# An LSTM step's four gates in one PSUM bank, with one sigmoid and one product for both pairs, in the steps that have FFN work

## The chip, the cores and the metric

The kernel runs on one core of a Trainium2 chip. The metric is the device time of one execution in microseconds. A core has a matrix engine (TensorE, PE in the profile, its weight loads PEld), VectorE (DVE), ScalarE (ACT), GpSimd (POOL) and SyncE (SP), which mostly issues DMAs. Matmul results land in PSUM, in banks of 512 fp32 elements per partition; TensorE writes them, VectorE and ScalarE read them.

## The reference

An LSTM with 256 units runs over 64 steps for 32 sequences, from h0 = `cond_1024`. Its output goes through three dense layers (256 → 1024 → 1024 → 256) whose weights are +1 or −1, and is added to the input `x`:

```python
def step(carry, xw_t):
    prev_h, prev_c = carry
    a = xw_t + prev_h @ Wh
    i = jax.nn.sigmoid(a[:, :Hd])
    f = jax.nn.sigmoid(a[:, Hd:2 * Hd])
    o = jax.nn.sigmoid(a[:, 2 * Hd:3 * Hd])
    g = jnp.tanh(a[:, 3 * Hd:])
    next_c = f * prev_c + i * g
    next_h = o * jnp.tanh(next_c)
    return ((next_h, next_c), next_h)
...
w = jnp.where(kernel_bool, jnp.float32(1.0), jnp.float32(-1.0))
...
x = x + ffn(lstm(x, cond_1024, Wx, Wh, b), k0, k1, k2, s0, s1, s2)
```

The first layer sees h and −h side by side, and the first two layers are followed by relu(.) * 2. All values are fp32.

## The kernel before

**Layout of a step.** The 256 units are cut into four quarters of 64. A tile of a step has 128 partitions, quarter by sequence (4 × 32), and 64 elements. The gates stand in the order candidate, input, forget, output (`GATES`, slots 0 to 3).

**Two stages.** The loop over `t` at the end of the function runs through the 64 steps. In each it issues the gate products (`gates_from_h`, L308), then the cell (`cell_step`, L325 to L342), and then a share of other TensorE work, written out by hand, that fills the time until the next h is there. Before step `X_STEPS` = 21 this is the input product x @ Wx for later steps (`x_products`, L249; results leave PSUM with the bias through L265 into `xg`). From step 21 on it is the FFN over blocks of 16 steps (`ffn`; matmuls at L425, L679, L666 and, for the last two blocks, L452), with 10 or 11 matmuls of 512 elements a step, set by `total_ffn` over the steps left. After step 63 the rest of the FFN runs without a recurrence beside it.

**A step's gates.** `gates_from_h` adds h @ Wh into two PSUM banks: the first three slots into one, 192 wide, the output gate into the other, 64 wide. In each bank there are 2 halves of the contraction by 4 quarters, each a matmul with 32 columns, fp32, which the trace shows as two passes. What is added to lies there already: `gates_from_x` has ScalarE copy the next step's input product into both banks (L319, L320), after the tanh of this step in ScalarE's order.

**A step's cell.** ScalarE: sigmoid of input and forget gate (L325), tanh of the candidate (L326), sigmoid of the output gate from the other bank (L327). VectorE: kept = forget × c (L329), new = input × candidate (L331), c = kept + new (L333). ScalarE: th = tanh(c) (L335). VectorE: h = output × th (L337), then the turn of h by 32 × 32 blocks into `hist` (L342), which the next step's gate products take as weights.

**What else the engines do.** Each engine executes in the order of the program. In FFN steps, behind the cell, ScalarE evicts FFN banks (L368 relu, L436, L437, L514 copy) and rounds h (L361), and VectorE forms the remainders that make the FFN's operands exact (L369, L438, L362), turns outputs (L392) and adds up weight blocks (L418). `load` keeps a count of a step's larger VectorE pieces. GpSimd and the DMAs have little to do after the first 20 us.

Of the kernel before, what the change touches and what calls it, by code (L numbers as in the profile page):

```python
# [34 lines left out]
F32 = mybir.dt.float32  # L35
F32R = mybir.dt.float32r
U8 = mybir.dt.uint8
AF = mybir.ActivationFunctionType
# [5 lines left out]
def lstm_ffn(ctx: ExitStack, tc: tile.TileContext, x, cond, wx_d, wh_d, b_d, k0_d, k1_d, k2_d, s0_d, s1_d, s2_d, out):  # L44
    nc = tc.nc
    P = 128
# [4 lines left out]
    HQ = H // NQ  # L51
# [11 lines left out]
    X_STEPS = 21  # L63
# [13 lines left out]
    cell = ctx.enter_context(tc.tile_pool(name="cell", bufs=2))  # L77
# [6 lines left out]
    def act(shape, dtype, name):  # L84
        return apool.tile(shape, dtype, tag="act", name=name)
# [77 lines left out]
    for i in range(2):  # L163
        t = act([P, 2, F0], U8, f"k0_{i}")
# [102 lines left out]
    def next_x(half):  # L267

        if half < 2 * NB:
            load[0] += 1  # L270
            turn_x(*divmod(half, 2))
            if half + 4 < 2 * NB:
                load_x(*divmod(half + 4, 2), [nc.sync])
# [25 lines left out]
    hist, hparts = {}, {}  # L299

    gate_banks = [ps_g.tile([P, TB], F32, tag=f"gates{n}", name=f"gates{n}") for n in (3, 1)]
    gates = [g[:, : n * HQ].rearrange("p (g j) -> p g j", j=HQ) for g, n in zip(gate_banks, (3, 1))]

    def gates_from_h(t, hT):
        for g, slots in zip(gates, (slice(0, 3), slice(3, 4))):
            for k in range(2):
                for q in range(NQ):
                    nc.tensor.matmul(  # L308
                        g[q * N : (q + 1) * N],
                        hT[:, k, :],  # L310
                        wh_q[:, k, q, slots],
                        start=False,
                        stop=(k == 1),
                        skip_group_check=True,
                    )

    def gates_from_x(t):
        x_t = xg[t // 2 * 2][:, t % 2].rearrange("p (g j) -> p g j", g=4)
        nc.scalar.copy(gates[0], x_t[:, :3])  # L319
        nc.scalar.copy(gates[1], x_t[:, 3:])  # L320

    def cell_step(t, c):
        sig = cell.tile([P, 3, HQ], F32, tag="sig", name=f"sig{t}")
        cand = cell.tile([P, HQ], F32, tag="cand", name=f"cand{t}")
        nc.scalar.activation(sig[:, 0:2, :], gates[0][:, 1:3], AF.Sigmoid)  # L325
        nc.scalar.activation(cand, gates[0][:, 0], AF.Tanh)  # L326
        nc.scalar.activation(sig[:, 2, :], gates[1][:, 0], AF.Sigmoid)  # L327
        kept = cell.tile([P, HQ], F32, tag="kept", name=f"kept{t}")
        nc.vector.tensor_mul(kept, sig[:, 1, :], c)  # L329
        new = cell.tile([P, HQ], F32, tag="new", name=f"new{t}")  # L330
        nc.vector.tensor_mul(new, sig[:, 0, :], cand)  # L331
        c = cell.tile([P, HQ], F32, tag="c", name=f"c{t}")
        nc.vector.tensor_add(c, kept, new)  # L333
        th = cell.tile([P, HQ], F32, tag="th", name=f"th{t}")
        nc.scalar.activation(th, c, AF.Tanh)  # L335
        h = cell.tile([P, HQ], F32, tag="h", name=f"h{t}")
        nc.vector.tensor_mul(h, sig[:, 2, :], th)  # L337
        i, s = divmod(t, SH)
        if s == 0:
            hist[i] = hpool.tile([P, 2, SH * N], F32, tag="hist", name=f"hist{i}")  # L340
        hT = hist[i][:, :, ts(s, N)]
        nc.vector.transpose(hT, h.rearrange("p (j b) -> p b j", b=2))  # L342
        if t + 1 < T:
            gates_from_x(t + 1)
        return c, hT

    def split_h(i):

        b, s = divmod(i, SB // SH)
        if s == 0:  # L350
            hparts[b] = (
                hpool.tile([P, 2, TB], F32R, tag="hhi", name=f"hhi{b}"),
                hpool.tile([P, 2, TB], F32R, tag="hlo", name=f"hlo{b}"),
            )
        hi, lo = (p[:, :, ts(s, SH * N)] for p in hparts[b])
        full = hist.pop(i)
        if b == NB - 1:

            hi, lo = (a.rearrange("p k (n t) -> p k t n", n=N) for a in (hi, lo))
            full = full.rearrange("p k (t n) -> p k t n", n=N)  # L360
        nc.scalar.copy(hi, full)  # L361
        nc.vector.tensor_tensor(lo, full, hi, ALU.subtract)  # L362
# [58 lines left out]
    f, parts = {}, {"b11": {}, "b21": {}}  # L421
# [291 lines left out]
    for half in range(2):  # L713
        load_x(2, half, [nc.sync])
    hT = const.tile([P, 2, N], F32, name="hT_first")
    c = cell.tile([P, HQ], F32, tag="c", name="c_first")
    nc.vector.memset(c, 0.0)  # L717

    def copy_bias():
        p_bias = ps_o.tile([P, 4, HQ], F32, tag="po", name="p_bias")  # L720
# [24 lines left out]
    for _ in x_products(SB // 2, AHEAD):  # L745
        pass
    gates_from_x(0)


    def ffn():  # L750
        for b in range(NB - 2):
            yield from ffn_block(b)
        yield from last_blocks(NB - 2)
# [13 lines left out]
    for t in range(T):  # L767
        load[0] = 0
        gates_from_h(t, hT)
        c, hT = cell_step(t, c)  # L770
        if t % SH == SH - 1:
            splits.append(t // SH)
        if outputs:
            load[0] += 1
            if next(outputs[0], "end") == "end":
                outputs.popleft()
        if t == X_STEPS:
            work, done = ffn(), 0
        goal = (t + 1) * total_x // X_STEPS if t < X_STEPS else (t + 1 - X_STEPS) * total_ffn // (T - X_STEPS)
        while done < goal:  # L780
            left_over[0] = goal - done
            done += next(work)
        if t == X_STEPS - 1:
            next(work, None)

        if turns and load[0] < 2:
            next_x(turns.popleft())
        if splits and (load[0] < 2 or t == T - 1 or t == SH * splits[0] + 2 * SH - 1):
            split_h(splits.popleft())
        else:  # L790
            if t >= FIRST_CHORE and chores:
                part = chores.popleft()()
                if part is not None:
                    w0_parts.append(part)
            elif t >= W2_STEP and chores2:
                chores2.popleft()()
            if w0_parts and (load[0] < 2 or t == X_STEPS - 1):
                w0_parts.popleft()()
            while sum_parts and t >= SUM_STEP and load[0] < 2:
                load[0] += 1  # L800
                sum_parts.popleft()()
# [32 lines left out]
```

## Time and profile before

| | us |
|---|---|
| runs of the kernel | 307.01, 307.42, 308.49 (median 307.42) |
| profiled execution | 307.09 |
| its span | 305.3 |
| PE busy | 299.3 |
| DVE busy | 187.8 |
| ACT busy | 154.9 |
| gate passes of 192 elements, 1008 (steps 1 to 63) | mean 0.330 |
| gate passes of 64 elements, 1008 | mean 0.219 |
| input-product passes of 256 elements, 880 | mean 0.379 |

Duration is from start to modelled end; passes overlap, so durations don't add up to time. A row of the timeline has start, length, engine, line, operation, what it writes and reads, and in brackets how long the engine had been idle before it and what ended that. A row of the chain has start, length and what carried it. The steps begin at 16.5 us (step 0), the FFN steps at 79.9, and the last step's gates at 231.4.

### The profile page before, as it was taken

The page shows a single profiled execution, that of the slowest core. Times are in us where ns is not written, and L with a number is a line of the kernel's source. Part 1 is how long each engine was busy: PE and PEld are TensorE (multiplying, and loading weights), DVE is VectorE, ACT ScalarE, POOL GpSimd, SP SyncE. Part 2 cuts the span into 40 slices and gives each one's busy share as a digit, 9 for nine tenths or more (in the row PEclk, how much of TensorE's full clock was granted, in tenths as well). Part 3 has the DMA queues.
Part 4 walks back from the last instruction along what each step waited for, and adds up shares of the span by engine and source line. Part 5 has one row for each costly group of instructions (what it writes and reads, how often), then busy time and mean ns, then how long its engine had stood idle before and what let it go on. Part 6 is the DMA issues. An engine that isn't in the chain of part 4 may idle for free.

```text
span 305.3 us, 9553 instructions
## 1 busy us (share of the span) xinstructions
PE 299.3 (98%) x4010; PEld 233.8 (77%) x4010; DVE 187.8 (62%) x527; ACT 154.9 (51%) x526; POOL 6.6 (2%) x24
## 2 busy tenths in 40 slices
PE   8999999999999999999999999999999999999993
PEld 4988887787777777777777777777777888888893
DVE  2476767676774565666575746444456689796341
ACT  0224657784565654444453544655676688644100
POOL 5300000000000000000000000000000000000000
PEclk9999999999999999999999999999999999999999
DMA  6865001133000000000001000000001330000012
GB/s 182 210 181 114 20 10 48 32 84 84 4 0 2 2 2 1 2 2 1 2 2 38 19 18 2 0 2 3 3 0 37 91 83 0 0 0 2 0 51 88
DMA packets 27450, 10.87 MB, mean 36 GB/s; under 512 B 23560, under 2 KB 26632, under 8 KB 27408
## 3 DMA queue, kind: packets, MB, share of 16 engines
q1 hardware_dynamic: 24768, 8.66, 11.5%
q10 hardware_dynamic: 2400, 1.57, 1.8%
q8 instruction: 31, 0.51, 0.7%
q0 software_dynamic: 240, 0.04, 0.1%
q14 instruction: 11, 0.09, 0.1%
HBM read 8.16 MB, written 2.10 MB: 34 GB/s over the span
## 4 chain that ended last, share of the span: by engine, by line
PE 98%; DVE 0%; issue 0%
PE p L679 21%; PE gates L308 20%; PE px L249 18%; PE q L452 12%; PE p L425 9%; PE po L666 5%; PE po L629 2%; PE gates L452 2%; PE po L617 2%; PE r L452 2%; PE gates L425 1%; PE p_idle L708 1%; PE gates L706 0%; DVE o L637 0%; PE p_bias L723 0%; DVE idle L113 0%
## 5 line engine op out<-in xcount | busy, mean ns | idle before, releaser
L308 PEld LDWEIGHTS gates<-wh,hist 128*32 128x32 f32 x2016 | 54.6, 109 | 22.3 <-issue 7.8
L308 PE MATMUL gates<-wh,hist 128*32 128x192 f32 x2016 | 68.1, 275 | 0.0
L249 PE MATMUL px<-wx,xT 128*32 128x256 f32 (+1 forms) x1168 | 60.5, 353 | 0.1
L249 PEld LDWEIGHTS px<-wx,xT 128*32 128x32 f32 x1168 | 42.4, 110 | 11.4 <-DVE c_first L717 0.8
L325 ACT ACTIVATE sig<-gates 128x128 f32<-128x128 f32 x64 | 17.7, 277 | 60.7 <-PE gates L308 60.4
L329 DVE TENSOR_TENSOR kept<-sig,c 128x64 f32<-128x64 f32 x63 | 14.2, 225 | 32.4 <-ACT sig L325 32.1
L335 ACT ACTIVATE th<-c 128x64 f32<-128x64 f32 x64 | 16.4, 257 | 32.2 <-DVE c L333 32.2
L337 DVE TENSOR_TENSOR h<-sig,th 128x64 f32<-128x64 f32 x64 | 14.4, 225 | 20.7 <-ACT th L335 20.7
L265 DVE TENSOR_TENSOR xg<-px,bias 128x512 f32<-128x512 f32 x32 | 21.2, 671 | 2.8 <-PE px L249 2.3
L425 PE MATMUL p<-hlo,w 128*128 128x512 f32 x56 | 22.5, 402 | 0.0
L425 PE MATMUL p<-hhi,w 128*128 128x512 f32 x56 | 22.3, 399 | 0.0
L319 ACT COPY gates<-xg 128x192 f32<-128x192 f32 x64 | 20.0, 313 | 0.6 <-DVE xg L265 0.6
L342 DVE STREAM_TRANSPOSE hist<-h 128x64 f32<-128x64 f32 x64 | 15.7, 246 | 2.6
L333 DVE TENSOR_TENSOR c<-kept,new 128x64 f32<-128x64 f32 x64 | 14.4, 225 | 2.2
L327 ACT ACTIVATE sig<-gates 128x64 f32<-128x64 f32 x64 | 14.9, 233 | 0.1
L331 DVE TENSOR_TENSOR new<-sig,cand 128x64 f32<-128x64 f32 x64 | 14.0, 218 | 0.0
L326 ACT ACTIVATE cand<-gates 128x64 f32<-128x64 f32 x64 | 14.0, 218 | 0.0
L320 ACT COPY gates<-xg 128x64 f32<-128x64 f32 x64 | 13.0, 203 | 0.0
L425 PEld LDWEIGHTS p<-hlo,w 128*128 128x128 f32 x56 | 10.5, 188 | 2.5
L425 PEld LDWEIGHTS p<-hhi,w 128*128 128x128 f32 x56 | 10.5, 188 | 2.4
L214 ACT ACTIVATE w<-bits,nsgn,sgn 128x1024 fp32r<-128x1024 uint8 x8 | 9.9, 1241 | 0.0
L362 DVE TENSOR_TENSOR hlo<-hist,hhi 128x256 fp32r<-128x256 f32 x16 | 7.5, 468 | 2.6 <-ACT hhi L361 2.6
(361 smaller groups left out, 573.4 us busy)
## 6 DMA issues: line engine op xcount, KB each, us to landing
x<-in_x_dram SPq DMA_DIRECT2D x52, 64.0 KB, 2.7
out_dram<-o SPq DMA_DIRECT2D x28, 64.0 KB, 1.8
bits<-in_L_ffn_k_dram SPq DMA_DIRECT2D x10, 128.0 KB, 3.4
wx<-in_L_cond_Wx_dram SPq DMA_DIRECT2D x2, 256.0 KB, 4.4
wx<-in_L_cond_Wx_dram ACTq DMA_DIRECT2D x4, 128.0 KB, 5.3
wh<-in_L_cond_Wh_dram ACTq DMA_DIRECT2D x2, 256.0 KB, 6.1
wh<-in_L_cond_Wh_dram SPq DMA_DIRECT2D x2, 256.0 KB, 6.8
k<-in_L_ffn_k_dram SPq DMA_DIRECT2D x2, 256.0 KB, 3.0
```

The costliest lines, as they stand in the source:

```text
L249: nc.tensor.matmul(p[q * N : (q + 1) * N, t % 2, slots], xT[i // 2, i % 2][:, s, k, :], wx_q[:, k, q, slots], start=start, stop=False, ski ...
L265: nc.vector.tensor_tensor(xg[t], p.rearrange("p t g j -> p t (g j)"), b, ALU.add)
L308: nc.tensor.matmul(g[q * N : (q + 1) * N], hT[:, k, :], wh_q[:, k, q, slots], start=False, stop=(k == 1), skip_group_check=True,)
L319: nc.scalar.copy(gates[0], x_t[:, :3])
L325: nc.scalar.activation(sig[:, 0:2, :], gates[0][:, 1:3], AF.Sigmoid)
L327: nc.scalar.activation(sig[:, 2, :], gates[1][:, 0], AF.Sigmoid)
L335: nc.scalar.activation(th, c, AF.Tanh)
L342: nc.vector.transpose(hT, h.rearrange("p (j b) -> p b j", b=2))
L425: nc.tensor.matmul(p, w0[:, k, ts(m, P)], a[:, k, :], start=(n == 0), stop=(n == 3))
L452: nc.tensor.matmul(bank, a(k)[:, ts(i, P)], b[k][n], start=first and k == 0 and n == 0, stop=k == K2 - 1 and n == 1, skip_group_check=True,)
L666: nc.tensor.matmul(po[m], w2[:, m, k], a1[k][n], start=(k == 0 and n == 0), stop=(k == FC1 - 1 and n == 1))
L679: nc.tensor.matmul(p1[m], w1[:, k, ts(m, P)], a0[k][n], start=(k == 0 and n == 0), stop=(k == FC0 - 1 and n == 1),)
```

## The change

It concerns the 43 steps from 21 on. There all four slots lie in the first of the two banks, 256 wide: `gates_from_h` issues 8 matmuls in place of 16, and `gates_from_x` one copy in place of two. The cell takes the tanh of the candidate first and then one sigmoid of input, forget and output gate, 192 wide. The candidate is written beside c, into a tile `pair` that the last step's c is in, so that one multiplication of 128 elements forms input × candidate and forget × c; the sum goes into the next `pair`. In steps 0 to 20 the two banks, three activations and two multiplications stay, with the results in `parts` and `pair`.

```diff
     gate_banks = [ps_g.tile([P, TB], F32, tag=f"gates{n}", name=f"gates{n}") for n in (3, 1)]
-    gates = [g[:, : n * HQ].rearrange("p (g j) -> p g j", j=HQ) for g, n in zip(gate_banks, (3, 1))]
+    rows, last_row = (g.rearrange("p (r j) -> p r j", j=HQ) for g in gate_banks)
+
+    def gate_parts(t):
+
+        if t < X_STEPS:
+            return (rows[:, :3], slice(0, 3)), (last_row[:, :1], slice(3, 4))
+        return ((rows[:, :4], slice(0, 4)),)
 
     def gates_from_h(t, hT):
-        for g, slots in zip(gates, (slice(0, 3), slice(3, 4))):
+        for g, slots in gate_parts(t):
...
-        nc.scalar.copy(gates[0], x_t[:, :3])
-        nc.scalar.copy(gates[1], x_t[:, 3:])
-
-    def cell_step(t, c):
+        for g, slots in gate_parts(t):
+            nc.scalar.copy(g, x_t[:, slots])
+
+    def cell_step(t, pair):
         sig = cell.tile([P, 3, HQ], F32, tag="sig", name=f"sig{t}")
-        cand = cell.tile([P, HQ], F32, tag="cand", name=f"cand{t}")
-        nc.scalar.activation(sig[:, 0:2, :], gates[0][:, 1:3], AF.Sigmoid)
-        nc.scalar.activation(cand, gates[0][:, 0], AF.Tanh)
-        nc.scalar.activation(sig[:, 2, :], gates[1][:, 0], AF.Sigmoid)
-        kept = cell.tile([P, HQ], F32, tag="kept", name=f"kept{t}")
-        nc.vector.tensor_mul(kept, sig[:, 1, :], c)
-        new = cell.tile([P, HQ], F32, tag="new", name=f"new{t}")
-        nc.vector.tensor_mul(new, sig[:, 0, :], cand)
-        c = cell.tile([P, HQ], F32, tag="c", name=f"c{t}")
-        nc.vector.tensor_add(c, kept, new)
+        parts = cell.tile([P, 2, HQ], F32, tag="parts", name=f"parts{t}")
+        cand, c = pair[:, 0], pair[:, 1]
+        if t < X_STEPS:
+            nc.scalar.activation(sig[:, 0:2, :], rows[:, 1:3], AF.Sigmoid)
+            nc.scalar.activation(cand, rows[:, 0], AF.Tanh)
+            nc.scalar.activation(sig[:, 2, :], last_row[:, 0], AF.Sigmoid)
+            nc.vector.tensor_mul(parts[:, 1], sig[:, 1, :], c)
+            nc.vector.tensor_mul(parts[:, 0], sig[:, 0, :], cand)
+        else:
+            nc.scalar.activation(cand, rows[:, 0], AF.Tanh)
+            nc.scalar.activation(sig, rows[:, 1:4], AF.Sigmoid)
+            nc.vector.tensor_mul(parts, sig[:, 0:2], pair)
+        pair = cell.tile([P, 2, HQ], F32, tag="pair", name=f"pair{t}")
+        c = pair[:, 1]
+        nc.vector.tensor_add(c, parts[:, 1], parts[:, 0])
...
-    c = cell.tile([P, HQ], F32, tag="c", name="c_first")
-    nc.vector.memset(c, 0.0)
+    pair = cell.tile([P, 2, HQ], F32, tag="pair", name="pair_first")
+    nc.vector.memset(pair, 0.0)
```

More of the change, by code (lines that the diff above doesn't have):

```diff
@@ L344, in cell_step @@
             gates_from_x(t + 1)
-        return c, hT
+        return pair, hT
     def split_h(i):
@@ L769, in lstm_ffn @@
         gates_from_h(t, hT)
-        c, hT = cell_step(t, c)
+        pair, hT = cell_step(t, pair)
         if t % SH == SH - 1:
```

## The prediction

> **What bounds the kernel now.** I read the page first, then the chain of waits, then the timeline of single steps. The page says who is full, the chain says what a step is made of, and the timeline says how much room there is beside it.
>
> ```profile
> PE 299.3 (98%) x4010; PEld 233.8 (77%) x4010; DVE 187.8 (62%) x527; ACT 154.9 (51%) x526; POOL 6.6 (2%) x24
> PE 98%; DVE 0%; issue 0%
> ```
>
> TensorE carries the chain from end to end, but a PE that is busy by its modelled ends can still be waiting a little, so the steps themselves decide. In order of time the chain shows two kinds of step:
>
> ```profile
> 34.97 0.87 PE gates L308 x32
> 35.84 2.16 PE px L249 x48
> ...
> 152.25 1.01 PE gates L308 x32
> 153.26 2.49 PE p L425 x10
> 155.75 1.01 PE gates L308 x32
> ```
>
> In the first a step is 0.87 us of gates and 2.16 of input products, in the second 1.01 us of gates and 10 or 11 FFN matmuls of 0.227. The change touches only the second kind, steps 21 to 63, 43 of them. Whether the recurrence (sigmoid to transposed h) is hidden there is read from one step, ScalarE's and VectorE's part of the timeline, with the next step's first weight load:
>
> ```profile
> 153.16 0.28 ACT L325 ACTIVATE sig<-gates 128x128 f32<-128x128 f32 x1 [1.81 <-PE gates L308]
> 153.34 0.22 ACT L326 ACTIVATE cand<-gates 128x64 f32<-128x64 f32 x1
> 153.44 0.23 ACT L327 ACTIVATE sig<-gates 128x64 f32<-128x64 f32 x1
> 154.13 0.26 ACT L335 ACTIVATE th<-c 128x64 f32<-128x64 f32 x1 [0.45 <-DVE c L333]
> ...
> 153.47 0.23 DVE L329 TENSOR_TENSOR kept<-sig,c 128x64 f32<-128x64 f32 x1 [1.66 <-ACT sig L325]
> 153.62 0.22 DVE L331 TENSOR_TENSOR new<-sig,cand 128x64 f32<-128x64 f32 x1
> 153.87 0.23 DVE L333 TENSOR_TENSOR c<-kept,new 128x64 f32<-128x64 f32 x1
> ...
> 154.68 0.25 DVE L342 STREAM_TRANSPOSE hist<-h 128x64 f32<-128x64 f32 x1
> ...
> 155.68 0.32 PEld L308 LDWEIGHTS gates<-wh,hist 128*32 128x32 f32 x12 [0.35 <-ACT a_4h L368]
> ```
>
> h is turned by 154.93 and is wanted at 155.68: 0.75 us of room. In the input-product steps the same two rows are 0.115 us apart, step after step (the turn ends at 61.62, the weights load at 61.73), so there the recurrence is the limit and 0.115 us is the shortest distance between them. The margin of the FFN step above is therefore 0.75 − 0.115 = 0.64 us. Read step by step, the distance is 0.75 where a step has 10 FFN matmuls, 0.98 where it has 11, and shorter in a few, least before steps 50, 53, 55 and 63 (0.34, 0.36, 0.29, 0.29). The short ones have one cause, work that is on VectorE already when the sigmoid is done:
>
> ```profile
> 182.21 0.68 DVE L418 TENSOR_TENSOR s<-w 128x512 fp32r<-128x512 f32 x1
> 182.80 0.22 DVE L329 TENSOR_TENSOR kept<-sig,c 128x64 f32<-128x64 f32 x1
> ```
>
> Here the sigmoid had been ready at 182.35, and kept started 0.45 us later. So in FFN steps TensorE's own work is the bound, the recurrence is not, and every other wait of TensorE there for ScalarE or VectorE (a bank to come free, a split operand) is met over 1 us early, up to the last step.
>
> **TensorE's part.** A gate matmul appears as two passes in the trace, on one of four strips of 32 columns, and four strips run side by side. Their starts, record by record: four passes of 192 elements follow the last four by 162.4 ns, of 64 by 55.8, and of 256 (the input products, same form of matmul) by 215.8. From 192 to 256 the 64 elements cost 53.4 ns, so a group of four has a fixed cost of 55.8 − 53.4 = 2.4 ns. A step has four groups of 192 and four of 64, 4 × 162.4 + 4 × 55.8 = 873 ns; after the change four of 256, 863 ns. The 16 passes that go, and their 16 weight loads, were beside the streaming already. That is 9.6 ns a step, 43 × 9.6 = **0.41 us**.
>
> The step's turn to the FFN matmuls is not the same after a 256-wide group, and the trace of before doesn't show that one. After the last group of 64 the next full-width weight load comes 168 ns after the group's start, 112 beyond its streaming; the other way, from a 512-wide FFN matmul to the gates, it is 317 ns, 101 beyond its 216. I take 112, which is what the same direction shows; 101 would save another 11 ns a step, 0.47 us, and nothing shows it longer.
>
> A rule speaks for far more. The Trainium skill, TensorEngine Tiling (Array Packing), Instruction Overhead, says that each matmul has about 60 cycles of overhead, so that one of 1 element is as slow as one of 60. By that, and the 2.4 GHz that its page TensorE: Matmul & The Clock Gate gives in its head, 16 passes fewer a step at 25 ns would be an estimated 0.4 us, 43 steps 17 us, and the time 290. The row for 64-wide passes, 55.8 ns for four, is 14 ns apiece and disagrees.
>
> **The recurrence's part.** What goes: the early start. Now L325 waits for the 192-wide group alone, whose last pass is modelled to end at 153.04, and starts 0.12 us later. With all gates in one bank the first activation waits for the last pass, which by the 215.8 spacing and the 379 ns of a 256-wide pass ends near 153.25, so cand starts near 153.38. Then, on ScalarE: sig may start 0.10 us behind cand, as L327 does behind L326, at 153.48. Its width of 192 is in no row for a sigmoid: 128 took 0.277 and 64 about 0.225, 0.81 ns an element, which makes 0.33 us; the copy of 192 took 0.31, and 0.28 + 0.23 in a row would be 0.51. I take 0.33: 153.81. On VectorE the one multiplication of 128 elements starts 0.03 later, at 153.84. It lies between 0.225 (64) and 0.468 (256, L362); at 1 ns an element, 0.29: 154.13, and the sum at 154.17, where it now starts at 153.87. From there on tanh, h and the turn are as before. **The chain grows by 0.30 us**, from 0.00 (if the multiplication hardly costs more than one now and sig overlaps cand more) to some 0.64 (sig 0.37, nothing overlapped, 0.47 for the multiplication).
>
> What hides it is the FFN matmuls of the step: 0.64 us of margin where there are 10, 0.87 where there are 11. Normal steps keep 0.34 us. In the short steps the lengthening is mostly not added: at 182.80 the multiplication would start when L418 lets go, as kept does, not when sig ends (182.72 by the same sum), and its sum 0.32 later instead of 0.39. If all 0.30 were added there, the four would overrun by 0.08, 0.06, 0.13 and 0.12 us, 0.39 in all. I take none and keep 0.39 for the range.
>
> The rest of ScalarE's work queues behind tanh: one copy of 256 elements instead of 192 and 64 (0.37 against 0.45 from start to end, with 0.93 us to spare), then the FFN evictions, up to 0.3 us later, whose readers have over 1 us. The tightest wait of the end, hlo of the last block at 236.67, has 0.06 us; but what sets it is L514, a copy that waits for TensorE until 234.79, while h of the last step is turned at 234.23, and 0.26 later does not move it. The DVE multiplication and the ACT instruction saved a step are off the path and worth nothing. Steps 0 to 20, where the recurrence does bound, keep their instructions, waits and order on each engine: kept and new write into one tile, but each waits for the same activation as before, and I cost them at zero. No DMA moves.
>
> **Sum.** The profiled execution was 307.09 us (span 305.3 and 1.8 around it): 307.09 − 0.41 = 306.68. The median of the runs is 307.42, 0.33 above it, and run to run they go from 307.01 to 308.49. From the median the sum gives 307.0, which is the forecast.
>
> **The rivals.**
> *The recurrence comes onto the path (slower).* It decides from a lengthening of 0.64 us on: beyond it each 0.01 us costs 0.01 in each of the 22 steps with 10 FFN matmuls, and from 0.87 on in all. At 0.75 it is 22 × 0.11 = 2.4 us, 309.4. For it: one engine after the other now waits for a wider instruction, VectorE is 62% busy, and blockers of 0.7 us stand ahead of it. Against it: all terms at their dearest only just reach 0.64, and blockers and lengthening overlap. 0.09.
> *The gates themselves are cheaper by more (faster).* If the 0.14 us by which an FFN step's gates exceed the others' (1.01 against 0.87) came from narrow passes at the turn and not from the turn, half of it gone would be 43 × 0.07 = 3.0 us, 304.0. For it: weight loads halve, and PEld is 77% busy. Against it: the same narrow passes cost nothing in the 0.87 us steps, and the turn's 112 ns is like the 101 after a wide one. 0.05.
> *Nothing but the fixed cost (same).* The forecast, 0.86, with its range from 306.2 (the shorter turn: 306.68 − 0.47) to 307.5 (0.39 of overruns on the median), widened by the runs' scatter to 306.0 and 308.5. Leaving both rivals out leaves 0.14 outside.
>
> A measurement of this kernel can tell about 0.5%, 1.5 us, from no change. Faster takes the second rival, 0.05, and a little of the scatter: 0.06; slower the first, 0.09, and as much: 0.10; within, 0.84.
>
> **What would show it.** Right: gates of 1.00 us in the chain's FFN steps, 16 passes, periods still 3.49 and 3.72; the turned h 0.45 us ahead of the weight load in a 10-matmul step; the first activation after the gates' end. Wrong: a distance of 0.115 in FFN steps, or the load of L308's weights waiting for the transpose there; gates under 0.95; or a changed period in steps 12 to 20.

## The result, and the profile after

The changed kernel is slower by 0.3%: 308.13 us median of 6 runs (307.70 to 308.47) against 307.02 for 6 runs of the kernel before (306.82 to 308.49), ratio 1.0031, 95% interval 1.0017 to 1.0046. Forecast was 0.41 us less. The profiled execution took 307.70 us (span 305.9) against 307.09 (305.3); the granted TensorE clock was 1.0 in both.

By stages, from the first weight load of a step's gates, in us:

| stage | before | after |
|---|---|---|
| gates of step 0 to gates of step 21 | 63.450 | 63.451 |
| gates of step 21 to gates of step 63 | 151.530 | 152.307 |
| gates of step 63 to the end | 73.830 | 73.802 |

The loss, 0.78 us, lies in the FFN steps alone. The chain of waits of the kernel after, the same steps as were shown of before:

```profile
152.45 1.00 PE gates L314 x16
153.45 2.53 PE p L436 x10
155.98 1.00 PE gates L314 x16
```

The gates went from 1.01 to 1.00 us, as forecast. But the 10 FFN matmuls between them, the same instructions as before, went from 2.49 to 2.53 (the chain of before is shown in the prediction). The recurrence is not in it. Here are its rows of the timeline in the kernel after, ScalarE, VectorE and the next step's first weight load:

```profile
153.57 0.22 ACT L339 ACTIVATE pair<-gates 128x64 f32<-128x64 f32 x1 [1.81 <-PE gates L314]
153.69 0.33 ACT L340 ACTIVATE sig<-gates 128x192 f32<-128x192 f32 x1
154.05 0.29 DVE L341 TENSOR_TENSOR parts<-sig,pair 128x128 f32<-128x128 f32 x1 [1.83 <-ACT sig L340]
154.38 0.22 DVE L344 TENSOR_TENSOR pair<-parts 128x64 f32<-128x64 f32 x1
...
155.19 0.25 DVE L353 STREAM_TRANSPOSE hist<-h 128x64 f32<-128x64 f32 x1
...
155.91 0.59 PEld L314 LDWEIGHTS gates<-wh,hist 128*32 128x32 f32 x16 [0.36 <-ACT a_4h L379]
```

h is turned at 155.44 and wanted at 155.91, 0.47 us of room against the 0.115 that a waiting step shows. Step by step the least of all FFN steps is 0.39, so TensorE never waits for h there.

What did change is seen in the timeline of PE, matmul by matmul. The kernel before, one step with 10 FFN matmuls:

```profile
153.19 0.50 PE L425 MATMUL p<-hlo,w 128*128 128x512 f32 x1
153.53 0.40 PE L425 MATMUL p<-hhi,w 128*128 128x512 f32 x1
153.76 0.39 PE L425 MATMUL p<-hlo,w 128*128 128x512 f32 x1
153.99 0.40 PE L425 MATMUL p<-hhi,w 128*128 128x512 f32 x1
154.22 0.39 PE L425 MATMUL p<-hlo,w 128*128 128x512 f32 x1
154.46 0.39 PE L425 MATMUL p<-hhi,w 128*128 128x512 f32 x1
154.68 0.39 PE L425 MATMUL p<-hlo,w 128*128 128x512 f32 x1
154.91 0.39 PE L425 MATMUL p<-hhi,w 128*128 128x512 f32 x1
155.13 0.39 PE L425 MATMUL p<-hlo,w 128*128 128x512 f32 x1
155.36 0.39 PE L425 MATMUL p<-hhi,w 128*128 128x512 f32 x1
```

The same step in the kernel after:

```profile
153.38 0.50 PE L436 MATMUL p<-hlo,w 128*128 128x512 f32 x1
153.72 0.40 PE L436 MATMUL p<-hhi,w 128*128 128x512 f32 x1
153.96 0.40 PE L436 MATMUL p<-hlo,w 128*128 128x512 f32 x1
154.19 0.40 PE L436 MATMUL p<-hhi,w 128*128 128x512 f32 x1
154.43 0.40 PE L436 MATMUL p<-hlo,w 128*128 128x512 f32 x1
154.66 0.39 PE L436 MATMUL p<-hhi,w 128*128 128x512 f32 x1
154.89 0.39 PE L436 MATMUL p<-hlo,w 128*128 128x512 f32 x1
155.12 0.40 PE L436 MATMUL p<-hhi,w 128*128 128x512 f32 x1
155.35 0.39 PE L436 MATMUL p<-hlo,w 128*128 128x512 f32 x1
155.58 0.40 PE L436 MATMUL p<-hhi,w 128*128 128x512 f32 x1
```

Read from the first column, start to start. From the records, in ns: before 336, 236, 228, 233, 231, then 226 or 227; after 341, 240, 235, 233, 236, 224, 231, 236, 228. In both the first distance holds the turn from the gates. Before the change the pace settles to 227 from the sixth matmul on; after the change it does not settle within the step. In what follows a step's **excess** is the sum of these distances less 227 apiece: 128 ns before, in steps of 10 and of 11 alike; after, 161 in most steps of 10 and 146 in most of 11. Where two numbers stand in the tables below, they are for these two. The length of the gates is taken from the first weight load of a step's gates to the start of its first FFN matmul.

That accounts for the loss. Over the 41 steps from 22 to 62: gates 41 × −0.010 = −0.41 us; first to last FFN start from 2.171 to 2.202 in the 22 steps of 10 and from 2.397 to 2.416 in the 19 of 11, 0.69 + 0.35; from the last FFN matmul to the next gates from 0.317 to 0.325 after the 22, 0.19. Together 0.81, with −0.03 in step 21: 0.78.

### The profile page after: what moved, and what is told of

Read it like the earlier page. It is cut to its first block, busy times and chain, and to the rows that moved or that the text cites. A ratio compares the mean times of both kernels' runs of the same rounds, so it can differ in the third digit from the quotient of the medians.

```text
span 305.9 us, 8015 instructions
## 1 busy us (share of the span) xinstructions
PE 300.0 (98%) x3322; PEld 217.6 (71%) x3322; DVE 185.1 (61%) x484; ACT 148.6 (49%) x440; POOL 6.6 (2%) x24
## 4 chain that ended last, share of the span: by engine, by line
PE 98%; DVE 0%; issue 0%
PE p L690 21%; PE gates L314 20%; PE px L249 18%; PE q L463 12%; PE p L436 9%; PE po L677 5%; PE po L640 2%; PE po L628 2%; PE r L463 2%; PE gates L463 2%; PE gates L436 1%; PE p_idle L719 1%; PE gates L717 0%; DVE o L648 0%; PE p_bias L734 0%; DVE idle L113 0%
## 5 line engine op out<-in xcount | busy, mean ns | idle before, releaser
L314 PE MATMUL gates<-wh,hist 128*32 128x256 f32 (+2 forms) x1328 | 67.7, 331 | 0.0
L314 PEld LDWEIGHTS gates<-wh,hist 128*32 128x32 f32 x1328 | 38.5, 109 | 24.5 <-issue 5.8
L346 ACT ACTIVATE th<-pair 128x64 f32<-128x64 f32 x64 | 16.4, 257 | 36.3 <-DVE pair L344 36.3
L339 ACT ACTIVATE pair<-gates 128x64 f32<-128x64 f32 x43 | 9.6, 224 | 46.3 <-PE gates L314 46.1
L341 DVE TENSOR_TENSOR parts<-sig,pair 128x128 f32<-128x128 f32 x43 | 12.5, 292 | 32.1 <-ACT sig L340 32.0
L326 ACT COPY gates<-xg 128x256 f32<-128x256 f32 (+1 forms) x85 | 25.3, 313 | 1.3 <-DVE xg L265 1.3
L344 DVE TENSOR_TENSOR pair<-parts 128x64 f32<-128x64 f32 x64 | 14.4, 225 | 2.2
L333 ACT ACTIVATE sig<-gates 128x128 f32<-128x128 f32 x21 | 5.8, 278 | 19.5 <-PE gates L314 19.4
L340 ACT ACTIVATE sig<-gates 128x192 f32<-128x192 f32 x43 | 14.0, 325 | 0.0
L372 ACT CAST hhi<-hist 128x256 fp32r<-128x256 f32 x16 | 7.5, 469 | 1.8 <-DVE hist L353 1.8
```

The source lines that it names most:

```text
L314: nc.tensor.matmul(g[q * N : (q + 1) * N], hT[:, k, :], wh_q[:, k, q, slots], start=False, stop=(k == 1), skip_group_check=True,)
L326: nc.scalar.copy(g, x_t[:, slots])
L344: nc.vector.tensor_add(c, parts[:, 1], parts[:, 0])
```

## Experiments

The question is why unchanged matmuls got slower. Theory 1: the form of the gates before them. Theory 2: the room, since TensorE's queue is held at the gates until h is there. Theory 3: the wider sigmoid and product disturb TensorE's reads. Intervals are of the ratio to the kernel before, and stage times are from the gates of step 21 to those of step 63.

### The parts alone

**One bank, old cell.** The changed kernel, whose FFN steps have the cell of before on the one bank:

```diff
-            nc.scalar.activation(cand, rows[:, 0], AF.Tanh)
-            nc.scalar.activation(sig, rows[:, 1:4], AF.Sigmoid)
-            nc.vector.tensor_mul(parts, sig[:, 0:2], pair)
+            nc.scalar.activation(sig[:, 0:2, :], rows[:, 1:3], AF.Sigmoid)
+            nc.scalar.activation(cand, rows[:, 0], AF.Tanh)
+            nc.scalar.activation(sig[:, 2, :], rows[:, 3], AF.Sigmoid)
+            nc.vector.tensor_mul(parts[:, 1], sig[:, 1, :], c)
+            nc.vector.tensor_mul(parts[:, 0], sig[:, 0, :], cand)
```

> Steps 21 to 63 have their gates in one bank, 256 wide, but the cell of before: two sigmoids, a tanh, two products. From the gates of step 21 to those of step 63 the kernel before took 151.53 us and the changed one 152.31, with gates 10 ns shorter a step; a step's 10 FFN matmuls took 2.171 from first to last start before and 2.202 after. Theory 1 (the form of the gates): four groups of 256 leave TensorE in a state in which the FFN matmuls behind them run slower; then this kernel has the 2.20 and about 152.3, whatever the cell. Theory 2 (the room): the FFN matmuls run slower because h is ready 0.3 us later, so that TensorE's queue is let go later; here the chain is longer by the lost early start alone, some 0.2 us, and the kernel lies between, 2.18 to 2.19 and 151.4 to 151.9. Theory 3 (contention): the wider sigmoid and the wider product disturb TensorE's reads; here neither is there, so 2.171 and 151.1.

Ratio 1.0026 (1.0014 to 1.0037); 152.308 us from step 21 to 63, 2.202 for 10 matmuls. The chain of this kernel:

```profile
152.91 1.00 PE gates L314 x16
153.91 2.53 PE p L438 x10
156.44 1.00 PE gates L314 x16
```

With the old cell, without a wider sigmoid or product, the whole loss is there: Theory 3 falls.

**Two banks, new cell.** The candidate first, one product for both pairs, two sigmoids since the gates lie in two banks:

```diff
-        if t < X_STEPS:
-            return (rows[:, :3], slice(0, 3)), (last_row[:, :1], slice(3, 4))
-        return ((rows[:, :4], slice(0, 4)),)
+        return (rows[:, :3], slice(0, 3)), (last_row[:, :1], slice(3, 4))
...
-            nc.scalar.activation(sig, rows[:, 1:4], AF.Sigmoid)
+            nc.scalar.activation(sig[:, 0:2, :], rows[:, 1:3], AF.Sigmoid)
+            nc.scalar.activation(sig[:, 2, :], last_row[:, 0], AF.Sigmoid)
```

> Two banks as before in all steps, but in steps 21 to 63 the candidate first, then the sigmoid of two gates, then that of the third, and the one product of 128 elements from the pair. The chain grows by about 0.1 us (the candidate ahead of the sigmoid, less the second product). Theory 1 (form of the gates): 2.171 us for 10 FFN matmuls and 151.53 from step 21 to 63, as before. Theory 2 (room): nearly as before, up to 151.8. Theory 3 (contention by wider instructions): the product of 128 is there, the sigmoid of 192 is not; part of the 0.03 us, 152 or more.

Ratio 1.0002 (0.9992 to 1.0012); 151.544 and 2.171. As Theory 1 has it.

**The kernel before with a longer chain.** One more multiplication, by a tile of ones, between c and its tanh.

```diff
+        late_c = c
+        if t >= X_STEPS:
+            late_c = cell.tile([P, HQ], F32, tag="late_c", name=f"late_c{t}")
+            nc.vector.tensor_mul(late_c, c, ones)
-        nc.scalar.activation(th, c, AF.Tanh)
+        nc.scalar.activation(th, late_c, AF.Tanh)
...
+    ones = const.tile([P, HQ], F32, name="ones")
+    nc.vector.memset(ones, 1.0)
```

> The kernel before, with one more multiplication by 1 (64 elements) between c and its tanh in steps 21 to 63, so that h is ready about 0.27 us later, with gates in two banks. Theory 1 (form of the gates): 2.171 us for 10 FFN matmuls and 151.53 from step 21 to 63, unchanged. Theory 2 (room): like the changed kernel, 2.20, and with the longer gates 152.7. Theory 3 (contention): nearly unchanged.

Ratio 1.0032 (1.0021 to 1.0043); 152.373 us, but with 2.172 for 10 matmuls and an excess of 128. So Theory 2's pace is not there. The time is lost in another way, which the chain of this kernel shows before step 53:

```profile
194.68 0.27 ACT th L339
194.97 0.24 DVE h L341
195.30 0.26 DVE hist L346
195.69 1.08 PE gates L308 x32
```

The chain leaves PE: the gates wait for the turned h, 0.115 us after it. The trace has this before steps 50, 53, 55, 62 and 63 (the longest waits before 53 and 63, 0.25 and 0.29 us), and the gates right behind a wait are 1.042 us long instead of 1.013 (1.08 and 1.01 in the chain, which counts a piece behind a wait from its weight load). None of the three expectations had it. It is the prediction's slower rival, here at work in the four steps that the prediction named and one more. The trace shows two ways in which VectorE's blockers, the work that stands ahead of the cell's first product, fail to absorb the delay. Before steps 50 and 55 kept starts where it did, 1.72 and 1.77 us behind the gates' first load, and the whole 0.26 us is added behind it. Before steps 53, 62 and 63 the blockers themselves come 0.24 to 0.26 us later, because the ScalarE pieces that they wait for queue behind the late tanh.

**The changed kernel without a recurrence.** The gates of steps 22 to 63 read the first h, and the copies for these steps, 42 of them by the trace, are left out.

```diff
-                        hT[:, k, :],
+                        (hT if t <= X_STEPS else hT_first)[:, k, :],
...
-        if t + 1 < T:
+        if t < X_STEPS:
             gates_from_x(t + 1)
```

> The changed kernel without a recurrence in steps 22 to 63: their gates come from the first h, and the input products are not copied in, so that no gate waits for h; all other instructions are there. It leaves out the recurrence and 43 copies of ScalarE. Theory 1 (form of the gates): the FFN matmuls stay slow, 2.20 for 10, and 152.3. Theory 2 (room): with all the room there is they run at least as in the kernel before, 2.171 or less, and 151.1 or less. Theory 3 (contention): slow as long as the wide instructions fall beside them, about 152.

Ratio 1.0029 (1.0017 to 1.0040); 152.301, 2.202, excess 161 and 146. The chain:

```profile
152.85 1.00 PE gates L314 x16
153.85 2.53 PE p L436 x10
156.38 1.00 PE gates L314 x16
```

With no h to wait for, nothing got better. Theory 2 falls. Theory 1 stands, with what counts in the form of the gates still open.

### What of the form

**The split of before in the one bank, and three other splits.** All keep the changed kernel's bank and cell; each list is (slots, half of the contraction) in the order of issue:

```diff
-        for g, slots in gate_parts(t):
-            for k in range(2):
+        parts = [(g, slots, k) for g, slots in gate_parts(t) for k in range(2)]
+        if t >= X_STEPS:
+            parts = [(rows[:, slice(*s)], slice(*s), k) for s, k in LIST]
+        for g, slots, k in parts:
+            # 192 and 64:      ((0, 3), 0), ((0, 3), 1), ((3, 4), 0), ((3, 4), 1)
+            # 64 and 192:      ((3, 4), 0), ((3, 4), 1), ((0, 3), 0), ((0, 3), 1)
+            # 128 and 128:     ((0, 2), 0), ((0, 2), 1), ((2, 4), 0), ((2, 4), 1)
+            # 256; 192 and 64: ((0, 4), 0), ((0, 3), 1), ((3, 4), 1)
```

> The changed kernel, one bank and its cell, but the gates of steps 21 to 63 are issued as before in matmuls of 192 and then of 64, into the one bank. It tells the bank from the form. If the bank or the cell slows the FFN matmuls: 10 of them 2.202 us from first to last start, and, with the longer gates, 152.7 from the gates of step 21 to those of step 63. If the form does (number of passes, or the width of the last ones): 2.171 and 151.5, as in the kernel before.

> As the last one, but the matmuls of 64 first and those of 192 after them. Number of passes and loads as in the kernel before, last passes wide. If the number counts (32 passes and 32 loads against 16): 2.171 and 151.5. If the width of the last passes counts: slow, 2.19 to 2.20 and 152.3 or more.

> One bank, the gates as matmuls of 128 and 128: 32 passes of one width. If the number counts: 2.171 and 151.5. If the width of the last passes counts: between before and changed, some 2.18 to 2.19 and 151.9.

> One bank; the first half of the contraction in matmuls of 256, the second in matmuls of 192 and then of 64: 24 passes, the last ones narrow. If the number counts: half way, 2.187 and 151.9. If the width of the last passes counts: 2.171 and 151.3, with gates 5 ns shorter than before.

| gates as | passes | gates, us | excess, ns | step 21 to 63, us | ratio |
|---|---|---|---|---|---|
| kernel before, 192 and 64 in two banks | 32 | 1.013 | 128 | 151.53 | |
| changed kernel, 256 | 16 | 1.003 | 161, 146 | 152.31 | 1.0031 (1.0017 to 1.0046) |
| 192, 64 | 32 | 1.012 | 128 | 151.50 | 0.9995 (0.9979 to 1.0010) |
| 64, 192 | 32 | 1.012 | 128 | 151.53 | 0.9989 (0.9978 to 1.0001) |
| 128, 128 | 32 | 1.013 | 128 | 151.54 | 1.0004 (0.9994 to 1.0013) |
| 256; 192, 64 | 24 | 1.007 | 142, 127 | 151.79 | 1.0009 (0.9995 to 1.0022) |

The chain of the first of them, to compare with the changed kernel's:

```profile
152.11 1.01 PE gates L317 x32
153.12 2.49 PE p L439 x10
155.61 1.01 PE gates L317 x32
```

One bank and the new cell cost nothing once the gates have their old split; neither the bank nor the width of the last passes is it. What is left looked like the number of passes.

**More passes.** 128, 64, 64 (48 passes), four times 64 (64 passes), and 16 passes of 2 elements ahead of or behind the changed kernel's:

```diff
+            # 48: ((0, 2), 0), ((0, 2), 1), ((2, 3), 0), ((2, 3), 1), ((3, 4), 0), ((3, 4), 1)
+            # 64: ((i, i + 1), k) for i in range(4) for k in range(2)
...
+            small = [(gate_banks[1][:, 384:386], None, k) for k in range(2)]
+            parts = small + parts   # or parts + small
...
-                        wh_q[:, k, q, slots],
+                        wh_q[:, k, q, 0, :2] if slots is None else wh_q[:, k, q, slots],
```

> The changed kernel, with 8 more matmuls of 2 elements (16 passes, 16 loads) ahead of the gates' own in steps 21 to 63, into columns of the second bank that nobody reads. If the number of passes before the FFN matmuls sets their pace: 2.171 us for 10 of them and 0.317 from the last to the gates, 39 ns a short step and 18 a long one less than in the changed kernel, against 16 passes more of 14 ns at most (0.05 to 0.06 us a step): 152.3 to 154 from step 21 to 63 by what a small pass costs. If the width or the time of the gates sets it: 2.202, and 154 to 155. Beside that it prices a pass of 2 elements: by streaming alone four would be some 4 ns, by the 64-wide row at most 56.

> The same 16 passes of 2 elements behind the gates' own. If the number counts: as with the small passes first. If it counts what stands last before the FFN matmuls: only this one has 2.171.

> The changed kernel with the gates as matmuls of 128, 64 and 64 into the one bank: 48 passes. Twelve groups, 2.4 ns each over the streaming, 10 ns a step more than with 32 passes. If the pace gets better with the number on from 16 over 24 to 32: 10 FFN matmuls in 2.16 us or less and 151.5 or less. If 32 is enough: 2.171, 151.9.

> The gates as four matmuls of 64 into the one bank: 64 passes, sixteen groups, gates 19 ns longer than with 32 passes. If more passes make a better pace: 2.15 us or less for 10 FFN matmuls (9 x 0.227 = 2.04 and the first, slow one, 0.11, are the floor), 151.5. If 32 is enough: 2.171 and 152.3.

| gates as | passes | gates, us | excess, ns | step 21 to 63, us | ratio |
|---|---|---|---|---|---|
| 2-wide, then 256 | 32 | 1.129 | 161, 146 | 157.63 | 1.0206 (1.0182 to 1.0229) |
| 256, then 2-wide | 32 | 1.102 | 125 to 152, 139 on average | 155.77 | 1.0138 (1.0118 to 1.0159) |
| 128, 64, 64 | 48 | 1.023 | 161, 146 | 153.15 | 1.0047 (1.0030 to 1.0064) |
| 64, 64, 64, 64 | 64 | 1.032 | 128 | 152.34 | 1.0025 (1.0015 to 1.0035) |

48 passes are as slow as 16 (both cases of that expectation missed), and 64 as fast as 32: more passes don't make it better, and 32 passes with small ones ahead of the others are slow. The two totals with small passes missed every expectation, because 16 passes of 2 elements took 126 and 99 ns instead of at most 60.

**The length of the gates.** The splits so far also differ by 10 ns in how long the gates take. Four runs hold the number of passes at 24 and change only the width of 8 unused ones ahead of the gates, W = 33, 36, 39, 42 (a pass has two rows of W, so 66 to 84 elements):

```diff
+            spare = gate_banks[1][:, 256 : 256 + 2 * W].rearrange("p (r j) -> p r j", r=2)
+            parts = [(spare, None, 0)] + parts
...
+                        wh_q[:, k, q, 2:4, :W] if slots is None else wh_q[:, k, q, slots],
```

> The changed kernel with 4 more matmuls (8 passes, two groups of four) of 66 elements ahead of the gates of steps 21 to 63, into columns that nobody reads: 24 passes, gates some 2 x (66 x 0.834 + 2.4) = 115 ns longer than in the changed kernel, about 1.118 us. The FFN matmuls of a step take 128 ns over 0.227 apiece in the kernel before and 161 or 146 (after 11 or 10) in the changed one. If the number of passes counts (modulo 32): as with 24 before, 127 to 142 in turn, in all four of these runs. If the moment counts: 1.118 is 0.105 over the first fast point (1.013), 5.4 times 19.3, so rather slow, and the four runs differ from each other in turn.

> The same with 72 elements: gates 10 ns longer, about 1.128 us. If the number counts: as the last one. If the moment counts, with a turn of about 20 ns: the opposite of the last one, 128 if that was slow.

> The same with 78 elements, about 1.138 us. If the number counts: as the last two. If the moment counts: as with 66.

> The same with 84 elements, about 1.148 us. If the number counts: as the others. If the moment counts: as with 72.

| width of the unused passes | gates, us | excess, ns | step 21 to 63, us | ratio |
|---|---|---|---|---|
| 66 | 1.117 | 136 | 156.25 | 1.0199 (1.0173 to 1.0225) |
| 72 | 1.127 | 142, 127 | 156.83 | 1.0196 (1.0180 to 1.0211) |
| 78 | 1.137 | 161, 167 | 158.61 | 1.0240 (1.0217 to 1.0262) |
| 84 | 1.147 | 142, 127 | 157.70 | 1.0223 (1.0208 to 1.0238) |

With equal numbers of passes, and the same 16 passes of 256 last before the FFN matmuls, the pace behind them differs. The number is out, and so is the width of the last passes as what alone decides. The expectation that every second one is alike held for 72 and 84 and failed for 66 and 78.

**The two kernels themselves, with their own numbers of passes.** Gates 10 ns shorter in the kernel before, and 7 ns shorter in the changed one:

```diff
+                    w = 58 if t >= X_STEPS and k == 1 and slots.start == 3 else HQ   # kernel before
+                    w = 63 if t >= X_STEPS and k == 1 else HQ                        # changed kernel
                     nc.tensor.matmul(
-                        g[q * N : (q + 1) * N],
+                        g[q * N : (q + 1) * N, :, :w],
                         hT[:, k, :],
-                        wh_q[:, k, q, slots],
+                        wh_q[:, k, q, slots, :w],
```

> The kernel before; in steps 21 to 63 the output gate's matmuls of the second half of the contraction are 58 wide instead of 64, which leaves out that half's part for 6 of each 64 units. 32 passes as before, two groups of four shorter by 6 x 0.834 = 5 ns each, gates 1.003 us, as long as in the changed kernel. If the length of the gates counts: the FFN matmuls of a step slow, 153 ns over 0.227 apiece as in the changed kernel, and 42 x (25 - 10) = 0.6 us more than before from step 21 to 63 (152.2). If the number of passes counts: 128, and 0.4 us less than before (151.1).

> The changed kernel; in steps 21 to 63 the matmuls of the second half of the contraction are 4 x 63 wide, which leaves out that half's part for the last of each 64 units. 16 passes, gates 2 x 4 x 0.834 = 7 ns shorter, 0.996 us. If the length counts: another pace than 153, towards 128 if it comes back every 19 to 20 ns (then 0.996 stands as 1.015 does, close behind the fast 1.013); some 151.2 to 152 from step 21 to 63. If the number of passes counts: 153 as before it, and 152.0.

The kernel before, shortened: ratio 1.0025 (1.0014 to 1.0037), gates 1.003, excess 161 and 146, 152.301 us. Its chain:

```profile
152.72 1.00 PE gates L309 x32
153.72 2.53 PE p L426 x10
156.25 1.00 PE gates L309 x32
```

This is the deciding run. Two banks, the old cell, 32 passes, and 10 ns less work in the gates: the FFN matmuls take the changed kernel's excess, 161 and 146, and the step gets longer. So no group of 256 is needed for it. The narrower passes, 58 for 64, went with the length here; but 192 and 64, 64 and 192, and 128 and 128, all 1.012 to 1.013 us long, kept 128. The changed kernel, shortened: 1.0021 (1.0008 to 1.0034), gates 0.996, excess still 161 and 146, 152.02 us; the guess that the pace comes back every 19 to 20 ns was wrong there.

## Why the prediction was wrong

**What bounds the kernel: right.** TensorE does, in FFN steps, and the recurrence keeps room: 0.475 us ahead of the gates in a step with 10 matmuls (forecast 0.45), 0.39 at least. Of the steps without FFN work the prediction read too much from one: h is 0.115 us ahead of the gates of steps 1 and 11 to 21 alone, and 0.19 to 0.20 ahead of those of 2 to 10. That cost nothing.

**The gates and the turn behind them: right.** 1.003 us against 1.013, the 9.6 ns from the fixed cost of a group of four. The first FFN weight load comes 328 ns after the last group's start, 112 beyond its 216, as taken. (The other way was read wrongly: 317 ns less the 227 at which 512-wide FFN matmuls settle is 90; no run shows 216 for these. It served for the range alone, whose upper end before scatter, 307.0 and 0.39, is 307.4 and not 307.5.) The rule of 60 cycles a matmul, which would have made 17 us of it, did not hold here.

**The chain: right.** The turned h stands 0.32 us later against the gates than before (0.30 forecast): sigmoid 0.325 (0.33), product 0.292 (0.29), first activation 0.13 behind the gates' end. In the blocked steps the lengthening was absorbed, as argued: the distances before steps 50, 53 and 55 were 0.44, 0.46 and 0.39, none below the 0.34, 0.36 and 0.29 of before. The kernel before with a late multiplication shows the other case: 0.84 us for 0.26 of lengthening. The prediction's 0.39 for such overruns was half of it; it left out step 62, the longer gates behind a wait, and that a late tanh can delay the blockers too.

**The steps without FFN work and the end: right.** 63.45 us in both; hlo of the last block ends as close before the matmul that reads it (0.07 us, 0.06 before).

**The sum: the step that failed.** "The step's turn to the FFN matmuls is not the same after a 256-wide group" was priced, and then "10 or 11 FFN matmuls of 0.227" were taken for what follows. For what follows the sum took no change, without a reason, and that is where it failed: the pace of those matmuls depends on what runs ahead of them, the length of the gates included. It costs 1.2 us where the gates save 0.41, and turned a forecast of 0.41 less into 0.78 more. The median of 308.13 us still lies between the 306.0 and 308.5 of the prediction, but by what was added there for overruns of the chain and for scatter; nothing there was for slower matmuls, so that is luck. The periods forecast as 3.49 and 3.72 were 3.530 and 3.735.

The trace of before had the sign of it. Its own chain, the first FFN steps and a later one:

```profile
81.18 2.52 PE p L425 x10
...
84.71 2.50 PE p L425 x10
...
153.26 2.49 PE p L425 x10
```

Ten equal matmuls, 2.52 us behind the gates of step 21 and 2.49 later. The records say 2.191, 2.180 and 2.171 us from first to last start, behind gates of the same instructions. I read the third and divided it; the first two say that the pace is not a constant of the matmul.

**The rivals.** Neither came. The recurrence did not reach the path, and the gates were not cheaper by more. The slower end was taken for an overrun of the chain, and its cause lay in TensorE itself.

**What stays open.** Shown is that 10 ns off the length of the gates, with bank, cell, number of passes and recurrence held, changes the pace of the FFN matmuls behind them. By which rule isn't shown. 0.996 and 1.003 us are slow, 1.007 in between, 1.012 fast, 1.023 slow, 1.032 fast; with the unused passes ahead, 1.117 and 1.137 differ, 1.127 and 1.147 do not.

The records order most of this by a short period. Measured from the changed kernel's, the lengths that differ by −6.8, 0, 20.1 and 126.5 ns, whole multiples of 6.67, have an excess of 161 and 146; those that differ by 9.8 to 10.0 and by 29.8, half a period beyond, have 128; those that differ by 4.9, 124.7 and 144.9, some 0.7 beyond, have 142 and 127 or 128. The 114.9 and 134.8 of the unused passes of 66 and 78 lie at 0.2 and are not alike. This is a fit made with all results known, and no run tested it; it would say why a guess of 19 to 20 ns, three such periods, held at some points.

Nor are the gates all of it. In the changed kernel, from step 23 on, a step of 10 has 161 when the step before had 11 matmuls and 142 when it had 10. In the kernel with 2-wide passes last, whose gates are 1.101 or 1.102 us long throughout, steps of 10 behind steps of 11 have 125 or 126 in some stretches and 148 in another. So something is carried over from step to step. That fits a pace that goes by the moment at which the matmuls start, which is argued and not shown; what in TensorE or in its reads makes it so, no run here can tell.

None of the 18 kernels beats the kernel before by more than its interval. The nearest is the one bank and the new cell with gates of 64 first and 192 after, 0.9989 (0.9978 to 1.0001).

## What to carry to other kernels

Where one engine carries the whole path, check that a price read from it is constant: compare the same instructions behind different neighbours, and in the first steps after a change of stage, before multiplying. A saving of 10 ns a step can be smaller than what the matmuls behind it lose by it, 33 ns in a step of 10 here, so try two or three splits of equal work instead of the one with the fewest instructions. And when unchanged instructions get slower, take the parts of the change one at a time until the smallest edit brings the loss about; here it was 6 columns less in 8 of 32 passes.

## What the runs showed of the hardware

- After a turn from 32-column strips to full-width matmuls of 512, the distances between starts run through one sequence in the kernel before and in the changed one, to within 1 ns in most steps: 240, 235, 233, 236, 224, 231, 236, 228, 233, 231 and then 227. Each enters it at its own place: the changed kernel at its first or, with a 229, at its second place, the kernel before at the third from the 224 on (236, 228, 233, 231, 227). Where it is entered goes with the length of the gates (1.003 and 1.013 us) and with the step before.
- Four 2-element passes side by side cost 25 ns (99 / 4) behind the gates and 31 (126 / 4) ahead of them, where streaming alone would be near 4 and four of 64 elements take 56. The Trainium skill, TensorE: Matmul & The Clock Gate, Back-to-back issue gap, puts the floor of a matmul at about 25 ns; these runs come near it, 25 and 31, if the floor is counted for the group of four strips and not for each pass; that it is this floor which sets them is not shown.
